# The message product of layer 3: the picks of s are summed before the gathered d rows arrive

## The chip, the cores and the metric

The kernel runs on one NeuronCore of a Trainium2 chip. The time is the device time of one execution in microseconds (us); for the kernel before it is the median of three runs, 1174.64 us (1171.81 to 1176.21). The engines are called PE (TensorE, with PEld for its weight loads), DVE (VectorE), ACT (ScalarE), POOL (GpSimd) and SP (SyncE, which issues most plain transfers).

## The reference, cut to what matters

Four layers run over a graph of 4096 nodes with 128 features, each as `x = x + layer(relu(layernorm(x)))`. The matrix `adj` is 4096 x 4096 and sparse, with uneven rows: a few nodes have many entries. Layers 0 to 2 (neighbour sum, Chebyshev filter, attention) multiply with it or a function of it. Layer 3 computes

```python
s = node_feats @ msg_w[:, :D].T
d = node_feats @ msg_w[:, D:].T
messages = gelu(s[:, None, :] + d[None, :, :] + msg_b)
aggregated = einsum('ijd,ij->id', messages, adj)
```

and then an update (a product, gelu, a layer norm). A message is needed only where `adj[i, j]` is not zero. The kernel makes, for each such entry (row i, column j), the vector `gelu(s_i + d_j)`, and adds it, times the entry's value, into row i.

## The kernel before, in words

**Tiling.** The nodes are put in an order on the host so that rows with many entries come first, and cut into 32 blocks of 128; four blocks are a group of 512 rows, with one PSUM bank as its accumulator. The entries of a block are listed in chunks of 128 entries. Blocks 0 and up have 26 (in four units of 7, 7, 7 and 5), 11, 8, 7, 6, 6, 5 and so on down to 3 chunks, 158 in all. A message of the program is up to four chunks of one unit, and there are 49 of them: two for every unit of 5 to 8 chunks, three for block 1, and one for each of the blocks 10 to 31.

**One message** is the generator `Messages.message`, with `Messages.rows` beside it:

1. `selection` makes a 0/1 matrix that picks, for each entry of a chunk, its row of s: ACT writes distances (L623), DVE compares them (L625), into a lane of `m_lanes`.
2. When s of the group is there (`prepare`), DVE makes `r`, one 128 x 128 tile per chunk (L1403), which will send each entry back to its row, times its value. `r` lives in `r_tiles`.
3. `rows` has POOL gather the rows of d by an indirect DMA (L553), one per chunk, from a table in HBM into the message's buffer `m`. The program waits for all of them (`yield here[q]`).
4. PE adds d and s in a bank: a product of the identity with the gathered rows (L1409, up to 512 columns at once), then one product per chunk with the selection and s (L1411).
5. ACT takes the gelu of the bank into `m` (L1415), and the bank is free.
6. PE multiplies with `r` into the group's accumulator (L1421), and `r` and `m` are free.

In the profile an f32 product on PE shows as two records, so L1409 has 98 and L1411 and L1421 have 316 each.

**A group** starts with `prepare` (s for its rows, L597 and L1370, the diagonal entries, and the accumulator opened by a product of zeros, L602, then L1386). It ends with `finish`: the accumulator is copied (L1433), multiplied with the update weights (L597, `upd_h_sb` and `upd_a_sb`), and goes through a bias (L1441), gelu (L1444) and norm (L1453, L1456, L1458, L1462) to the output. Group 0, with the blocks that have most entries, sums in one of the two `picks` banks, the others in `accs`.

**Buffers.** While layer 2's attention runs there are three `banks`, four message buffers, one selection lane and two r tiles; only messages of block 0 run, at a low rank. When the attention is through, eight halves of its buffers become message buffers (twelve in all), and there are four lanes, four r tiles and one bank more. The d table is written group by group by `finish_3`, when two stripes of the attention are done: a transposition (L588), a product (L597, `msg_d_sb`), a copy and a store. Messages of blocks 1 and up need the whole table.

**The order of the work.** The kernel has no loops at run time. Its parts are Python generators; a planner (`Plan`) lets them go on one at a time, by when they could begin and by rank. A line such as `yield "PE", n * 0.84` asks for an engine with an expected duration (PE's are scaled by 0.72), `yield banks` asks for a buffer, and `yield here[q]` waits for an event, here the expected landing. The code behind the `yield` is then written into the program, and `in_order` keeps each engine's instructions in the planned order. What an engine does on the chip waits for its data in that order. Where the plan has a gap of over 0.8 us on PE and a bank has been free, `fill` puts in products of zeros (L610), up to 80% of the gap.

Of the kernel before, what the change touches and what calls it, by code (L numbers as in the profile page):

```python
# [26 lines left out]
D = 128  # L27
# [4 lines left out]
GB = BANK // D  # L32
# [334 lines left out]
def on_act(n, table=None):  # L367
    return ("ACT", 0.22 + 0.83e-3 * n) + ((table,) if table else ())
# [10 lines left out]
def sparse_stack(tc, x, adj, adjT, diag, w_self, w_neigh, b0, w1, b1, w2, att_src, att_dst,  # L379
# [7 lines left out]
    nc = tc.nc  # L387
    plan = Plan()
    EARLY = 7
    with ExitStack() as ctx:  # L390
# [4 lines left out]
        def tiles(pool, name, n, shape, dtype=F32):  # L395
            return Slots([pool.tile(list(shape), dtype, name=f"{name}{i}", tag=f"{name}{i}") for i in range(n)])

        def kept(name, shape, dtype=F32):
            return keep.tile(list(shape), dtype, name=name, tag=name)
# [17 lines left out]
        banks = tiles(ps, "bank", 3, (P, BANK))  # L417
# [25 lines left out]
        ident = kept("ident", (P, P))  # L443
# [156 lines left out]
        def open_bank(p):  # L600

            nc.tensor.matmul(p, nothing[0:1, :P], nothing[0:1, :], start=True, stop=False)  # L602
# [9 lines left out]
        def rows_of(p, n=GB):  # L612
            return p[:, :n * D].rearrange("p (k d) -> p k d", d=D)
# [6 lines left out]
        def selection(lane, mids, h, g, n):  # L620

            yield on_act(n * P)
            nc.scalar.activation(lane["t"][:, :n * P], iota_row[:, :n * P], AF.Abs, bias=mids[:, g:g + 1])  # L623
            yield on_dve1(n * P)
            nc.vector.tensor_scalar(lane["sel"].rearrange("p q e -> p (q e)")[:, :n * P], lane["t"][:, :n * P], h, None,  # L625
                                    op0=ALU.is_le)
# [690 lines left out]
        class Messages:  # L1317
# [76 lines left out]
            def message(self, g, b, u, c, chunks, m, here):  # L1394
                n = len(chunks)
                yield u_done[u.number]
                lane = yield m_lanes
                yield from selection(lane, mids[:, u.number, :], half[:, u.number:u.number + 1], c, n)
                yield self.s_here[g]
                r = yield r_tiles  # L1400
                yield "DVE", 0.35 * n
                for q, k in enumerate(chunks):
                    nc.vector.tensor_scalar(r[:, q, :], iota_row[:, :P], e_row[:, k:k + 1], e_val[:, k:k + 1],  # L1403
                                            op0=ALU.is_equal, op1=ALU.mult)
                for q in range(n):
                    yield here[q]
                p = yield banks
                yield "PE", n * 0.84
                nc.tensor.matmul(p[:, :n * D], ident, m[:, :n, :], start=True, stop=False)  # L1409
                for q in range(n):  # L1410
                    nc.tensor.matmul(p[:, q * D:(q + 1) * D], lane["sel"][:, q, :], self.s_rows[g][:, b % GB, :],  # L1411
                                     start=False, stop=q == n - 1)
                plan.release(m_lanes, lane)
                yield on_act(n * D, "gelu")
                nc.scalar.activation(m[:, :n, :], rows_of(p, n), AF.Gelu)  # L1415
                plan.release(banks, p)
                yield "PE", 0.42 * n
                acc = self.acc[g]
                for q in range(n):
                    self.left[b] -= 1  # L1420
                    nc.tensor.matmul(acc[:, b % GB * P:(b % GB + 1) * P], m[:, q, :], r[:, q, :], start=False,  # L1421
                                     stop=all(self.left[g * GB + k] == 0 for k in range(GB)))
                plan.release(r_tiles, r)
                plan.release(messages, m)
                if all(self.left[g * GB + k] == 0 for k in range(GB)):
                    plan.start(self.finish(g), -2)
# [160 lines left out]
        for i in range(2):  # L1587
            def lane_tile(name, width, dtype=F32):
                return second.tile([P, width], dtype, name=f"{name}_{i}", tag=f"{name}_{i}")
            lane = {k: lane_tile(k, -(-most // 2) + 2 * GB) for k in ("et", "ev", "epop", "ecum", "evf")}  # L1590
# [3 lines left out]
            n = max(sum(u.cap for u in g.units) for g in GROUPS)  # L1594
# [23 lines left out]
        def message_lanes(pool, numbers):  # L1618
            return [{"t": pool.tile([P, BANK], F32, name=f"mt{i}", tag=f"mt{i}"),
                     "sel": pool.tile([P, GB, P], F32, name=f"msel{i}", tag=f"msel{i}")} for i in numbers]  # L1620
# [11 lines left out]
        m_lanes = Slots(message_lanes(early, range(1)))  # L1632
# [365 lines left out]
```

## Time and profile before

| what | value |
|---|---|
| median of three runs | 1174.64 us |
| the profiled execution | 1485.49 us |
| its span | 1483.4 us, mean clock 0.842 |
| PE busy (share of the span) | 1055.1 us (71%) |
| DVE, ACT, POOL busy | 792.7, 671.2, 766.4 us (53%, 45%, 52%) |
| zero products that open a bank (L602, from 985 us) | 20, median 384 ns |
| zero products that fill (L610, 1205 to 1445 us) | 120, median about 379 ns |
| gathers of d rows (L553) | 158 |

The profiled execution is 311 us longer than the median; its durations of single instructions and its order are used here, and a difference of times is set against its own time first. Times are counted from the start of the span. In the tables an idle time before an instruction is followed by what ended it: "issue" is a wait for nothing that the profile shows, "remote" one for something outside the core. Tile names are those of the program: a message's buffer appears as `m`, or as `e` or `tau` where it is a half of an attention buffer, and a bank as `bank` or `pick`.

### The profile page before, as it was taken

What the parts mean: (1) busy time and instruction counts of PE and PEld (TensorE: products, weight loads), DVE (VectorE), ACT (ScalarE), POOL (GpSimd) and SP (SyncE); (2) the same over time, 40 slices, a digit from 0 to 9 for tenths busy, and PEclk for the clock granted to TensorE, in tenths of its full rate; (3) what the DMA queues carried; (4) which work ended last, traced back from release to release, by engine and by line L of the source; (5) the groups of instructions that cost most, each with busy time, mean ns of one, the idle gap of its engine ahead of it and who ended that gap; (6) DMA issues with size and microseconds to landing.
All of it is one profiled execution on the core that took longest, in us unless ns stands there. A gap on an engine that the chain in (4) does not pass through costs nothing.

```text
span 1483.4 us, 19188 instructions
## 1 busy us (share of the span) xinstructions
PE 1055.1 (71%) x5943; PEld 722.2 (49%) x5943; DVE 792.7 (53%) x2982; ACT 671.2 (45%) x1344; POOL 766.4 (52%) x832
## 2 busy tenths in 40 slices
PE   6786778877486687667677069968767872957774
PEld 2454556554265465455555045534434452645663
DVE  5796567787466476345645048444444451424453
ACT  5983466664021213113335048656555630334366
POOL 4136664344635565546656733765557346664530
PEclk9897799897697899778888579979888995988988
DMA  8999899895565777766544034333333212112210
GB/s 252 357 329 334 286 299 330 305 353 185 135 185 147 211 228 227 201 187 181 150 115 132 8 93 132 107 88 89 88 107 97 61 50 49 42 42 53 61 45 24
DMA packets 175415, 236.03 MB, mean 159 GB/s; under 512 B 22452, under 2 KB 155336, under 8 KB 167112
## 3 DMA queue, kind: packets, MB, share of 16 engines
q1 hardware_dynamic: 148904, 186.45, 37.8%
q0 software_dynamic: 26400, 48.27, 13.6%
q8 instruction: 49, 0.80, 0.2%
q14 instruction: 62, 0.51, 0.1%
HBM read 203.41 MB, written 31.23 MB: 158 GB/s over the span
## 4 chain that ended last, share of the span: by engine, by line
PE 23%; another core or an unknown queue 13%; ACT 10%; DVE 7%; issue 6%; DMA 1%; POOL 0%; ACTq 0%; SPq 0%; DVEq 0%; POOLq 0%
PE acc L1253 4%; PE acc L1255 3%; PE bank L597 2%; PE acc L1421 2%; PE acc L1139 2%; PE acc L1156 2%; ACT junk L1453 1%; ACT e L1229 1%; ACT junk L568 1%; PE bank L1411 1%; PE pick L610 1%; ACT e L1232 1%; PE bank L1409 1%; DVE ehit L891 1%
## 5 line engine op out<-in xcount | busy, mean ns | idle before, releaser
L553 POOL DMA_INDIRECT e_val<-in_adj,e_at x158 | 154.5, 978 | 48.0 <-issue 45.6
L553 POOL DMA_INDIRECT g<-h_tab,fetch_row x136 | 136.1, 1001 | 73.0 <-issue 34.3
L610 PE MATMUL pick<-nothing 128*128 128x512 f16 x536 | 142.9, 416 | 1.6 <-issue 1.6
L1139 PE MATMUL acc<-big,hA 128*128 128x256 f32 x448 | 131.7, 442 | 10.7 <-issue 7.7
L610 PEld LDWEIGHTS <-nothing 128*128 128x128 f16 x795 | 82.9, 107 | 99.3 <-issue 33.4
L553 POOL DMA_INDIRECT g<-a_tab,fetch_col x74 | 76.9, 1039 | 93.6 <-issue 45.3
L553 POOL DMA_INDIRECT rseg<-in_adjT,seg_row x68 | 71.1, 1046 | 103.4 <-issue 28.8
L1139 PEld LDWEIGHTS acc<-big,hA 128*128 128x128 f32 x448 | 96.4, 225 | 28.6 <-issue 9.5
L553 POOL DMA_INDIRECT cseg<-in_adj,seg_col x74 | 70.8, 957 | 63.9 <-issue 23.2
L891 DVE SCALAR_TENSOR_TENSOR ehit<-ehit,pos,pick 128x32 f32<-128x32 f32 (+7 forms) x158 | 38.8, 285 | 116.0 <-issue 80.1
L1236 DVE TENSOR_TENSOR tau<-e,big 128x512 f32<-128x512 f32 (+3 forms) x61 | 54.3, 891 | 85.5 <-ACT e L1232 47.8
L553 POOL DMA_INDIRECT g<-u_tab,fetch_row x68 | 64.6, 950 | 64.9 <-PE acc L1156 37.1
L888 ACT COPY ehit<-pick 128x192 f32<-128x192 f32 (+7 forms) x74 | 20.4, 286 | 154.5 <-remote 80.4
L553 POOL DMA_INDIRECT tau<-d_tab,e_col x63 | 60.6, 962 | 57.2 <-issue 15.0
L769 ACT ACTIVATE mask<-dst 128x2048 fp8e4<-128x2048 f32 x43 | 81.8, 1903 | 14.2 <-DMA dst<-in_adj 8.0
L553 POOL DMA_INDIRECT m<-d_tab,e_col x70 | 68.4, 977 | 38.5 <-issue 17.4
L1156 PE MATMUL acc<-big,g 128*128 128x256 f32 x272 | 80.2, 434 | 0.6 <-DMA big<-r_tab 0.5
L568 ACT ACTIVATE junk<-xN,stat 128x128 f32<-128x128 f32 x128 | 51.4, 401 | 60.0 <-DVE stat L564 27.0
L623 ACT ACTIVATE sel_t<-iota_row,mids 128x512 f32<-128x512 f32 (+3 forms) x43 | 27.1, 642 | 109.7 <-DVE mids L618 63.7
L610 PE MATMUL bank<-nothing 128*128 128x512 f16 x259 | 70.6, 414 | 2.7 <-issue 2.3
L884 PE MATMUL pick<-eA,esel 128*128 128x65 f16 (+7 forms) x158 | 27.0, 245 | 61.4 <-DVE esel L625 28.0
L1139 PE MATMUL acc<-big,hB 128*128 128x256 f32 x224 | 62.7, 420 | 1.7 <-DMA big<-in_adjT 1.7
(331 smaller groups left out, 2717.2 us busy)
## 6 DMA issues: line engine op xcount, KB each, us to landing
dst<-in_adj SPq DMA_DIRECT2D x43, 1024.0 KB
big<-in_adjT SPq DMA_DIRECT2D x45, 512.0 KB
raw<-in_adj SPq DMA_DIRECT2D x21, 1024.0 KB
big<-in_adjT SPq DMA_DIRECT2D x66, 256.0 KB
big<-r_tab SPq DMA_DIRECT2D x30, 512.0 KB
c_tab<-cseg SPq DMA_DIRECT2D x74, 128.0 KB
r_tab<-rseg SPq DMA_DIRECT2D x68, 128.0 KB
big<-c_tab SPq DMA_DIRECT2D x15, 512.0 KB
```

The lines of the kernel that those rows point to most:

```text
L553: nc.gpsimd.indirect_dma_start(out=dst, out_offset=None, in_=table[:, :], in_offset=bass.IndirectOffsetOnAxis(ap=index, axis=0))
L568: nc.scalar.activation(junk, src[:, k, :], AF.Square, bias=st[:, 0, k:k + 1], accum_out=st[:, 1, k:k + 1])
L597: nc.tensor.matmul(p[:, k * D:(k + 1) * D], lhs[:, k * P:(k + 1) * P], w, start=i == 0, stop=i == len(terms) - 1)
L610: nc.tensor.matmul(idle[2][idle[1]], nothing[:, :P], nothing, start=True, stop=True)
L769: nc.scalar.activation(mask[:, h * HALF:(h + 1) * HALF], raw_of[b, h], AF.Sigmoid, scale=1e38, accum_out=marks[:, 2 * b + h:2 * b + h + 1] ...
L891: nc.vector.scalar_tensor_tensor(hit[:, q, :], hit[:, q, :], pos0[:, k + q:k + q + 1], pv[:, q, W:2 * W], op0=ALU.is_le, op1=ALU.mult, acc ...
L1139: nc.tensor.matmul(acc, self.near[:, b, :D], as_rows(t)[:, k, :], start=count == 0, stop=count == every - 1)
L1156: nc.tensor.matmul(acc, row[:, :D], r, start=count == 0, stop=count == every - 1)
L1236: nc.vector.tensor_mul(tau[:, :n, :], e[:, :n, :], a[:, :n, :])
L1253: nc.tensor.matmul(acc[0:1, CS:2 * CS], parts[k][:, D + 1:], tau[:, k, :], start=False, stop=False)
L1255: nc.tensor.matmul(acc[:, :CS], parts[k][:, :D], e[:, k, :], start=False, stop=self.count[s.index] == every - 1)
L1421: nc.tensor.matmul(acc[:, b % GB * P:(b % GB + 1) * P], m[:, q, :], r[:, q, :], start=False, stop=all(self.left[g * GB + k] == 0 for k in ...
```

## The change

In `message`, the bank is asked for right behind `r`, ahead of the wait for the gathered rows. A product of zeros opens it (`open_bank`, the function that opens the accumulators), the products with s are added, and the selection lane is given back. Then the message waits for the gathers, and the product of the identity with the gathered rows comes last. The durations that the planner is told are split: `n * 0.42 + 0.22` for the first part and `n * 0.42` for the second.

```diff
+                p = yield banks
+                yield "PE", n * 0.42 + 0.22
+                open_bank(p)
+                for q in range(n):
+                    nc.tensor.matmul(p[:, q * D:(q + 1) * D], lane["sel"][:, q, :], self.s_rows[g][:, b % GB, :],
+                                     start=False, stop=False)
+                plan.release(m_lanes, lane)
                 for q in range(n):
                     yield here[q]
-                p = yield banks
-                yield "PE", n * 0.84
-                nc.tensor.matmul(p[:, :n * D], ident, m[:, :n, :], start=True, stop=False)
-                for q in range(n):
-                    nc.tensor.matmul(p[:, q * D:(q + 1) * D], lane["sel"][:, q, :], self.s_rows[g][:, b % GB, :],
-                                     start=False, stop=q == n - 1)
-                plan.release(m_lanes, lane)
+                yield "PE", n * 0.42
+                nc.tensor.matmul(p[:, :n * D], ident, m[:, :n, :], start=False, stop=True)
                 yield on_act(n * D, "gelu")
```

`open_bank`, which is not changed:

```python
def open_bank(p):
    nc.tensor.matmul(p, nothing[0:1, :P], nothing[0:1, :], start=True, stop=False)
```

## The prediction

> **What bounds the kernel now.** I read the page's busy times first, then a table by stage, then the order of time on GpSimd (POOL), TensorE (PE) and ScalarE (ACT) in the stages that the edit touches. The first part of the page:
>
> ```profile
> PE 1055.1 (71%) x5943; PEld 722.2 (49%) x5943; DVE 792.7 (53%) x2982; ACT 671.2 (45%) x1344; POOL 766.4 (52%) x832
> ```
>
> No engine is full over the span, so the limits are local. Messages run from about 985 us; three stretches of layer 3 after the attention, from the table by stage (stretch, length, then busy us of PE, PEld, DVE, ACT, POOL, clock, DMA):
>
> ```profile
> 1207.00:1300.00 93.00, 58.31 (x308) 40.60 (x306) 21.19 (x66) 13.67 (x28) 60.19 (x63) 0.80 0.20 48
> 1300.00:1360.00 60.00, 34.86 (x188) 27.84 (x187) 20.22 (x56) 18.57 (x38) 35.67 (x38) 0.80 0.20 50
> 1360.00:1445.00 85.00, 67.13 (x388) 53.30 (x387) 42.98 (x123) 47.20 (x103) 36.44 (x38) 0.88 0.20 52
> ```
>
> A gather keeps POOL for 0.94 us with 0.30 us to the next, a pitch of 1.25. At that pitch the 63 gathers of the first row need 79 of 93 us, the 38 of the last 47.5 of 85. So the gathers set the pace at first and are behind something else at the end. What that is, POOL's order of time says:
>
> ```profile
> 1209.17 0.95 POOL L553 DMA_INDIRECT tau<-d_tab,e_col  x1 [0.30 <-issue]
> ...
> 1369.88 0.98 POOL L553 DMA_INDIRECT m<-d_tab,e_col  x1 [6.86 <-PE acc L1421]
> ...
> 1394.08 1.27 POOL L553 DMA_INDIRECT e<-d_tab,e_col  x1 [7.54 <-PE acc L1421]
> ...
> 1418.15 1.37 POOL L553 DMA_INDIRECT tau<-d_tab,e_col  x1 [7.43 <-PE acc L1421]
> ```
>
> A message buffer comes back only with the closing product L1421, and that is late once per group of four blocks. ACT shows the period, by the table load inside each group's norm:
>
> ```profile
> 1363.51 1.28 ACT L1456 ACT_TABLE_LOAD   x1
> ...
> 1387.40 1.28 ACT L1456 ACT_TABLE_LOAD   x1
> ...
> 1411.58 1.28 ACT L1456 ACT_TABLE_LOAD   x1
> ...
> 1434.12 1.28 ACT L1456 ACT_TABLE_LOAD   x1
> ```
>
> 23.9, 24.2 and 22.5 us apart, where a group's 12 gathers need 12 x 1.25 = 15. So the last groups go round a loop through ACT, PE and DVE, and PE's order inside one turn is:
>
> ```profile
> 1390.99 2.07 PE L1386 MATMUL acc<-r,own 128*128 128x128 f32 x8 [4.52 <-ACT own L1377]
> 1393.01 2.08 PE L1421 MATMUL acc<-r,e 128*128 128x128 f32 x8
> 1394.88 2.68 PE L1421 MATMUL acc<-r,tau 128*128 128x128 f32 x12
> 1397.39 0.81 PE L1409 MATMUL bank<-tau,ident 128*128 128x384 f32 x2
> ```
>
> After that come L1411 (s, six records, 0.66 us to the next) and at 1398.71 the update product L597, which ACT's norm waits for. Earlier, where gathers pace, one message is a d product, s products, fillers, closing product:
>
> ```profile
> 1265.23 1.02 PE L1409 MATMUL bank<-tau,ident 128*128 128x512 f32 x2
> 1266.09 1.05 PE L1411 MATMUL bank<-s,msel 128*128 128x128 f32 x8
> 1266.98 0.81 PE L610 MATMUL bank<-nothing 128*128 128x512 f16 x3
> 1267.83 1.16 PE L1421 MATMUL pick<-r,tau 128*128 128x128 f32 x8
> 1268.82 1.02 PE L1409 MATMUL bank<-m,ident 128*128 128x512 f32 x2
> ```
>
> From start to start: d 0.86, s 0.89, fillers 0.85, closing 0.99, in all 3.59 us for four chunks, against 5.0 us of POOL. An f32 product has two records here: 98 records of L1409 are 49 messages, 316 of L1411 are 158 chunks.
>
> **What the Trainium skill says.** "TensorE: Matmul & The Clock Gate", Part 1, What's actually happening: the array falls to half clock after about 3.4 us of idleness and recovers after as much work. The trace agrees: eight records of L1421 take 1.16 us at 1267.83, and 2.08 at 1393.01 behind a wait of 4.52. So a lost filler can cost as well as save. The same page, Back-to-back issue gap: 512 columns take 512/2.4 + 2.5 = 216 ns warm; 48 fillers take 10.52 us from 1205.90, 219 ns each. "PSUM — Partial Sum Buffer", The four PSUM rules, rule 2: the first product of a group clears the bank's written bits and later ones add; so the zero product lets s and d come in either order. No time in this trace tests that; the accumulators are opened in that way (L602).
>
> **The change part by part.** *Added:* 49 zero products. L602 is the same form, 20 of them with a median of 384 ns: 49 x 0.384 = 18.8 us of PE; bounds 49 x 0.219 = 10.7 (warm, back to back) and 49 x 0.602 (the longest L602) = 29.5. I take 18.8. Most lies in waits for gathers or in place of fillers (L610, 120 records from 1205 to 1445); without that cover it is all cost.
>
> *Moved:* the s products, from behind the gathers' landing to right behind DVE's r (L1403). From landing to gelu a message has 0.89 us (four chunks) or 0.66 (three) less. While POOL paces, this gains nothing: 12 message buffers let POOL run ahead, and PE needs 3.59 + 0.38 = 3.97 of 5.0 us. The s products queue in PE ahead of other messages' d and closing products, and now stand next behind r: three r take 0.85 us on DVE (1394.44 to 1395.3). No DMA is moved, no wait is added on SP or POOL.
>
> *Freed earlier:* the selection lane. Before the attention ends there is one lane, held through the wait for d. With it free the second early message's selection leaves DVE's queue at the end of the attention: 0.29 (L625) + 0.86 (three L1403, from 1187.83), and 0.40 for the third's, ahead of the last stripe's L1284 at 1191.68. That stripe ends in the last d rows, which hold POOL to 1207.92: -1.5 us.
>
> *Held longer:* the bank. Two r tiles before the attention ends mean that two of three banks sit open from about 1000 to 1180 us and the stripes' endings share one. Where two banks overlap in the trace, the later product waits for the earlier one's reader: L1277 at 1114.41 for ACT L590 to 1116.39 (2.0), L588 at 1145.72 for DVE L1288 to 1147.44 (1.7), L588 at 1179.19 for L1288 to 1180.11 (0.9). 4.6 us; PE has idle time there (164.9 busy of 205), so I take +2, bounds 0 and 4.6. Afterwards four r tiles stand against four banks.
>
> *The turn of the late loop.* When the closing products of three messages release their r tiles (1393 to 1397.5), DVE makes three new r at once, and the written order can put three openings and three s sets before L597: 3 x (0.38 + 0.66) = 3.1, less 0.66 for the L1411 that leaves: +2.5 us before the product that ACT waits for. What falls away behind L597 lies beside ACT's norm and gains nothing. Bounds per turn: -0.7 (s all in the wait before L1386) and +3.1. I take +2.5 in four turns: +10.
>
> *The tail.* From 1442.05 PE runs nearly without a break to 1454.3 through seven messages. With four r tiles up to four s sets leave (4 x 0.66 = 2.6) and three openings stay (1.1): about -1.
>
> Sum: 10 + 2 - 1.5 - 1 = +9.5 us. The profiled execution took 1485.49 us (span 1483.4), 311 us above the median of 1174.64; much of that seems to be waits without a visible cause (13% "another core or an unknown queue", 6% "issue" in the chain), so it would go to 1495. I carry the difference over unscaled: 1184 us.
>
> **Rivals.** *Hidden.* POOL's gathers (158 x 1.25 = 197.5 us) hold the pace once the stalls of the profile are gone, PE has room, the early bank conflicts vanish in PE's idle time: -1.5 - 1 + 2 = -0.5 and 1174 us. For it: 3.97 us against 5.0. Against it: the 7 us waits of POOL for L1421. That the planner has no bank free and puts s behind the landing as before ends here too.
>
> *Faster.* In the late loop s goes into the 4.5 us in which PE waits for ACT's own (1386.5 to 1391), and each message's path is shorter by 0.66: four turns x four messages x 0.66 = 10.6, 1164 us. It decides where the order puts s ahead of L1386 instead of L597; two of four turns bring it to the forecast's zero. Against it: the r tiles come free only behind L1386, in L1421.
>
> *Short of banks.* Four waiting messages hold all four banks when a group ends; its ending and the next group's prepare wait for a landing and a gelu, up to three gathers = 3.75 us in each of seven groups: +26, 1200 us. It decides where the fourth message has its r before the ending asks for a bank; the copy of the accumulator (0.58) is shorter than three r (0.85), which speaks against it.
>
> **How the numbers follow.** Forecast 0.38 (own range 1180 to 1194), short of banks 0.07, hidden 0.31, faster 0.24. A change below 0.5%, 5.9 us, can hardly be told from none here. Slower 0.45, same 0.31, faster 0.24. The written order is made anew by the planner from all its due times, so orders elsewhere in layer 3 shift too; this is in the widths. The range reaches to the faster case with three more us, and to the bank shortage: 1161 to 1200.
>
> **What would show it.** Right: 49 more zero products near 0.38 us, L1411 ahead of L1409 in each message; two or three L1411 sets between the last L1421 of a group and L597; table loads L1456 about 2.5 us further apart; fewer L610. Wrong: the same spacing of L1456 (hidden); L1411 inside the wait before L1386 and shorter waits of POOL for L1421 (faster); PE waits of 3 us and more in L597 for ACT's L1415 (banks). The forecast fails if the unprofiled loop is shorter than 15 us a group, since then POOL hides all of it.

## The result, and the profile after

The changed kernel takes 1183.49 us (median of 15 runs, 1178.67 to 1188.91). The kernel before, run beside it, takes 1175.98 us (15 runs, 1171.81 to 1183.72). The ratio is 1.0055, 95% interval 1.0037 to 1.0073: 0.55% slower, some 6.5 us (4.4 to 8.6). Every ratio here leaves out runs more than 1.5% above the fastest run of their kernel; that leaves out hardly any on the chips of usual speed, but many on the slow chips further down, where times spread more widely.

The profile of before that the prediction used is of an execution 311 us above the median. The unchanged kernel was therefore profiled again: 1179.77 us, span 1177.9 us, clock 0.938. The changed kernel's profile has a span of 1181.4 us and a clock of 0.932. All comparisons with "before" below use this second trace of it. Its page begins

```profile
PE 979.2 (83%) x5943; PEld 672.0 (57%) x5943; DVE 794.9 (67%) x2982; ACT 672.2 (57%) x1344; POOL 771.3 (65%) x832
```

and the changed kernel's page begins

```profile
PE 990.0 (84%) x5901; PEld 671.5 (57%) x5901; DVE 792.8 (67%) x2982; ACT 672.6 (57%) x1344; POOL 764.7 (65%) x832
```

PE does 10.8 us more. There are 49 more zero products of one row (L602: 88 records against 39, together 34.4 us against 15.6) and fewer fillers (L610: 704 records against 795). No other engine's busy time differs by more than 7 us. Behind the diff the lines of the changed kernel have moved: the s product is L1409, the d product L1415, the gelu L1417, the closing product L1423, the norm's table load L1458, the memsets that clear the attention's buffers L1648 (L1411, L1409, L1415, L1421, L1456 and L1646 before).

The stages after the attention, from the table by stage of the changed kernel (stretch, length, busy us of PE, PEld, DVE, ACT, POOL, clock, DMA share, GB/s):

```profile
980.00:1060.00 80.00, 66.49 (x367) 44.07 (x367) 33.92 (x102) 27.90 (x58) 60.51 (x64) 0.96 0.26 61
1060.00:1120.00 60.00, 52.96 (x325) 38.47 (x325) 34.11 (x96) 37.53 (x80) 45.67 (x48) 1.00 0.28 69
1120.00:1150.00 30.00, 29.60 (x189) 21.69 (x187) 20.51 (x62) 21.99 (x50) 22.99 (x24) 1.00 0.31 80
```

POOL issues 64 gathers in 80 us, 48 in 60 and 24 in 30: one every 1.25 us, up to the last. In the profile on record the last of these stages had 38 gathers in 85 us. POOL's order of time in the changed kernel:

```profile
957.95 0.93 POOL L553 DMA_INDIRECT e<-d_tab,e_col  x1 [0.30 <-issue]
976.53 0.94 POOL L553 DMA_INDIRECT tau<-d_tab,e_col  x1 [17.65 <-DVE own L1375]
977.78 0.95 POOL L553 DMA_INDIRECT tau<-d_tab,e_col  x1 [0.30 <-issue]
```

One wait stands in it, of 17.65 us, for the last rows of the d table. It ends with the first of the last 137 gathers, and none of the 136 others has a wait of over 0.31 us before it. So the late loop of the recorded profile, with its 7 us waits for the closing product, is absent at this kernel's usual time. It is absent before the change too (one wait of 10.71 us, the same 137 gathers behind it). The table loads of the late groups' norms in the changed kernel agree:

```profile
1095.94 1.28 ACT L1458 ACT_TABLE_LOAD   x1
1113.68 1.28 ACT L1458 ACT_TABLE_LOAD   x1
1129.44 1.28 ACT L1458 ACT_TABLE_LOAD   x1
1145.41 1.28 ACT L1458 ACT_TABLE_LOAD   x1
```

They are 17.7, 15.8 and 16.0 us apart; the same four before are 17.0, 17.0 and 17.0 apart. No such lengthening as the +2.5 us a turn of the prediction is seen. In both kernels 12 to 14 gathers fall between two of these loads, at 1.25 us each: the groups go at the pace of the gathers. A piece of PE's order between them shows the new message:

```profile
1100.98 0.38 PE L602 MATMUL bank<-nothing 1*128 1x512 f16 x1
1101.29 0.94 PE L1409 MATMUL bank<-s,msel 128*128 128x128 f32 x6
1102.06 0.83 PE L1423 MATMUL acc<-r,tau 128*128 128x128 f32 x6
1104.08 0.88 PE L1415 MATMUL bank<-m,ident 128*128 128x384 f32 x2 [1.18 <-DMA m<-d_tab,e_col]
1104.80 0.83 PE L1423 MATMUL acc<-r,tau 128*128 128x128 f32 x6
```

The opening and the s products do stand ahead of the gathered rows, in 1.1 us that PE partly spent waiting before. But PE waits for a gather there in either kernel, so nothing is gained.

**Where the loss is.** The last rows of d come from the attention's last stripe. Its chain in the kernel before, in order of time over the engines:

```profile
939.36 0.49 PE L1277 MATMUL bank<-ident,agg 128*128 128x128 f32 x2 [0.27 <-ACT agg L1272]
940.92 0.17 DVE L1284 RECIPROCAL stat<-bank 128x2 f32<-128x2 f32 x1 [1.67 <-PE bank L1278]
943.44 1.06 ACT L1232 ACTIVATE e<-e 128x1024 f32<-128x1024 f32 x1
944.53 1.23 DVE L1236 TENSOR_TENSOR tau<-e,big 128x1024 f32<-128x1024 f32 x1 [2.79 <-ACT e L1232]
946.54 1.89 PE L1253 MATMUL acc<-tau,g 128*1 128x256 f32 x8
947.08 2.11 DVE L1646 MEMSET e<- 128x512 f32 x4
...
955.27 0.17 DVE L1284 RECIPROCAL stat<-bank 128x2 f32<-128x2 f32 x1
957.06 0.40 ACT L568 ACTIVATE junk<-xN,stat 128x128 f32<-128x128 f32 x1 [2.42 <-DVE stat L564]
962.68 0.60 ACT L1415 ACTIVATE m<-bank 128x512 f32<-128x512 f32 x1
963.17 1.64 ACT L578 ACTIVATE hA<-xN,stat 128x128 f32<-128x128 f32 x4
964.32 0.87 PE L588 MATMUL bank<-ident,hA 128*128 128x128 f32 x4
966.82 1.16 PE L597 MATMUL pick<-msg_d_sb,hT 128*128 128x128 f32 x8 [0.73 <-ACT hT L590]
968.02 0.58 ACT L1305 COPY agg<-pick 128x512 f32<-128x512 f32 x1 [0.76 <-PE pick L597]
971.53 0.95 POOL L553 DMA_INDIRECT tau<-d_tab,e_col  x1 [10.71 <-DVE n_bad L1524]
```

A stripe's sums (L1253, then L1255) are turned by a transposition (L1277) and divided (L1284). L1277 and the first L1284 are those of the stripe before the last, the second L1284 is that of the last. L1232 is the attention's last exponential (the last exp below), L1236 makes from it what the last stripe's products L1253 read. Behind the last L1284 come the norm (L568, L578), the transposition (L588), the product that makes d (L597), the copy, the store, and 2.9 us after the store the first gather. The same chain in the changed kernel:

```profile
943.16 1.06 ACT L1232 ACTIVATE e<-e 128x1024 f32<-128x1024 f32 x1
944.25 1.23 DVE L1236 TENSOR_TENSOR tau<-e,big 128x1024 f32<-128x1024 f32 x1 [5.76 <-ACT e L1232]
946.65 0.49 PE L1277 MATMUL bank<-ident,agg 128*128 128x128 f32 x2 [0.75 <-ACT m L1417]
946.79 1.03 DVE L1648 MEMSET e<- 128x512 f32 x2
948.11 1.89 PE L1253 MATMUL acc<-tau,g 128*1 128x256 f32 x8
951.23 0.48 DVE L1648 MEMSET e<- 128x512 f32 x1 [3.41 <-PE acc L1255]
...
954.66 0.11 DVE L1284 RECIPROCAL stat<-bank 128x2 f32<-128x2 f32 x1
957.77 0.17 DVE L1284 RECIPROCAL stat<-bank 128x2 f32<-128x2 f32 x1
959.54 0.40 ACT L568 ACTIVATE junk<-xN,stat 128x128 f32<-128x128 f32 x1 [4.65 <-DVE stat L564]
963.67 1.64 ACT L578 ACTIVATE hA<-xN,stat 128x128 f32<-128x128 f32 x4
965.22 1.32 ACT L623 ACTIVATE mt<-iota_row,mids 128x512 f32<-128x512 f32 x2
966.55 1.28 ACT L1417 ACT_TABLE_LOAD   x1
967.85 0.98 ACT L1417 ACTIVATE m<-bank 128x512 f32<-128x512 f32 x2
968.50 1.12 PE L588 MATMUL bank<-ident,hA 128*128 128x128 f32 x4 [5.12 <-ACT m L1417]
971.12 1.86 PE L597 MATMUL bank<-msg_d_sb,hT 128*128 128x128 f32 x8
973.01 0.58 ACT L1305 COPY agg<-bank 128x512 f32<-128x512 f32 x1 [2.77 <-PE bank L597]
976.53 0.94 POOL L553 DMA_INDIRECT tau<-d_tab,e_col  x1 [17.65 <-DVE own L1375]
```

Three things have changed. First, the transposition L1277 of the stripe before the last waits for a bank that a block-0 message's gelu still reads; before, it ran at 939.36. It now stands in PE's order right ahead of the last stripe's L1253, which starts 2.6 us after the end of its input L1236; before it was 0.8 us. Second, the earlier stripe's L1284 now stands in DVE's order behind the memsets, some of which wait for the attention's last products (L1255), and beside two sets of r. Together the two make the last stripe's L1284 2.50 us later on the clock of the trace, and L568 with it. Third, ACT now does two selections, a table load and a gelu between L578 and the point where L588 gets its bank. L588 starts 4.83 us after L578 (968.50 - 963.67), where it took 1.15 us (964.32 - 963.17). Before, the gelu stood ahead of L578, which gives back 2.0 us of that. L597 then needs 1.86 us in place of 1.16 behind the wait. The store of the last rows starts at 973.62 instead of 968.63, 5.0 us later.

In these two executions the span's difference is 3.5 us: +5.0 at the store, +0.7 from the last gather to the end (31.4 against 30.7 us), and -2.2 in the gathers between, whose durations differ a little.

### The profile page after: what moved, and what is told of

It is laid out like the page before. It is cut to its first block, busy times and chain, and to the rows that moved or that the text cites. A ratio compares the mean times of both kernels' runs of the same rounds, so it can differ in the third digit from the quotient of the medians.

```text
span 1181.4 us, 19107 instructions
## 1 busy us (share of the span) xinstructions
PE 990.0 (84%) x5901; PEld 671.5 (57%) x5901; DVE 792.8 (67%) x2982; ACT 672.6 (57%) x1344; POOL 764.7 (65%) x832
## 4 chain that ended last, share of the span: by engine, by line
DMA 30%; PE 25%; ACT 13%; DVE 12%; POOL 9%; issue 8%; SPq 0%; POOLq 0%; ACTq 0%; DVEq 0%
DMA dst<-in_adj 5%; POOL e_val L553 4%; DMA cseg<-in_adj,seg_col 4%; PE acc L1139 3%; DMA g<-h_tab,fetch_row 3%; PE acc L1156 3%; PE bank L597 3%; ACT mask L769 3%; POOL g L553 3%; DMA e_val<-in_adj,e_at 3%; PE pick L610 2%; DMA big<-in_adjT 2%; DMA g<-a_tab,fetch_col 2%; ACT junk L568 2%; DMA m<-d_tab,e_col 2%
## 5 line engine op out<-in xcount | busy, mean ns | idle before, releaser
L553 POOL DMA_INDIRECT e_val<-in_adj,e_at x158 | 158.5, 1003 | 48.0 <-issue 40.1
L610 PE MATMUL pick<-nothing 128*128 128x512 f16 x514 | 132.5, 406 | 0.0
L1139 PE MATMUL acc<-big,hA 128*128 128x256 f32 x448 | 118.6, 410 | 8.7 <-DMA big<-in_adjT 5.8
L610 PEld LDWEIGHTS <-nothing 128*128 128x128 f16 x704 | 72.0, 105 | 80.7 <-issue 18.7
L553 POOL DMA_INDIRECT rseg<-in_adjT,seg_row x68 | 67.0, 985 | 74.9 <-issue 27.4
L1139 PEld LDWEIGHTS acc<-big,hA 128*128 128x128 f32 x448 | 88.5, 206 | 22.4 <-DMA big<-in_adjT 6.6
L553 POOL DMA_INDIRECT m<-d_tab,e_col x76 | 73.3, 965 | 23.2 <-issue 15.2
L553 POOL DMA_INDIRECT tau<-d_tab,e_col x63 | 60.8, 965 | 36.6 <-DVE own L1375 17.7
L1236 DVE TENSOR_TENSOR tau<-e,big 128x512 f32<-128x512 f32 (+3 forms) x61 | 54.3, 891 | 41.1 <-ACT e L1232 38.8
L568 ACT ACTIVATE junk<-xN,stat 128x128 f32<-128x128 f32 x128 | 51.3, 401 | 44.0 <-DVE stat L564 32.3
L1156 PEld LDWEIGHTS acc<-big,g 128*128 128x128 f32 x272 | 53.2, 209 | 27.5 <-DMA g<-h_tab,fetch_row 10.0
L1229 ACT ACTIVATE e<-dst,g 128x256 f32<-128x256 f32 x74 | 34.9, 501 | 38.7 <-DMA g<-a_tab,fetch_col 38.2
```

What stands on the lines that cost most here:

```text
L553: nc.gpsimd.indirect_dma_start(out=dst, out_offset=None, in_=table[:, :], in_offset=bass.IndirectOffsetOnAxis(ap=index, axis=0))
L568: nc.scalar.activation(junk, src[:, k, :], AF.Square, bias=st[:, 0, k:k + 1], accum_out=st[:, 1, k:k + 1])
L610: nc.tensor.matmul(idle[2][idle[1]], nothing[:, :P], nothing, start=True, stop=True)
L1139: nc.tensor.matmul(acc, self.near[:, b, :D], as_rows(t)[:, k, :], start=count == 0, stop=count == every - 1)
L1156: nc.tensor.matmul(acc, row[:, :D], r, start=count == 0, stop=count == every - 1)
L1229: nc.scalar.activation(e[:, k, :], dst[:, s.lo:s.lo + CS], AF.Relu, bias=h[:, D:D + 1])
```

## Experiments

Theory A (the prediction): the loss arises in the late groups, where s sets stand ahead of the update product. Theory B, formed from the changed kernel's trace: it arises at the end of the attention, where block-0 messages hold banks in which they have only summed s. Three more: the zero products themselves cost; holding a bank early costs whatever the order; or the time goes into the tail, from the last gather to the end. Ratios are to the kernel before on the same chip.

**before_look**: the kernel before, unchanged, to have a trace at its usual time.

> The kernel before, unchanged, profiled again for a trace that stands near its median. Late-loop theory (the prediction's): POOL still waits some 7 us for L1421 in each of the last groups, so the last gather of d rows ends late because of PE, ACT and DVE. Attention theory: POOL gathers without such waits, as in the changed kernel, and the gathers behind the full d table start 5 to 7 us before the changed kernel's 976.5. Tail theory: they start within 2 us of it, and from the end of the last gather to the end of the span there are 5 to 7 us less than the changed kernel's 31.4.

Measured: 1179.77 us; the readings are those above. The late loop isn't there. The first gather behind the whole table starts 5.0 us before the changed kernel's, as theory B had it, and the tail is 0.7 us shorter, not 5 to 7.

**zero_only**: the kernel before, its bank opened by the product of zeros, in place.

```diff
-                nc.tensor.matmul(p[:, :n * D], ident, m[:, :n, :], start=True, stop=False)
+                open_bank(p)
+                nc.tensor.matmul(p[:, :n * D], ident, m[:, :n, :], start=False, stop=False)
```

> The kernel before with the zero product put in front of d and s, at the same place and with the same expected durations, so that the order of all else is that of before. If PE's 49 x 0.384 = 18.8 us stand on the path: 5 us and more above before, so 1181 and up. If they lie beside the gathers (attention theory, tail theory): within 2 us of before, 1174 to 1178.

Measured: 1177.99 against 1177.74 us, ratio 1.0009 (0.9988 to 1.0031). The 49 zero products (88 records of L602, 34.5 us together) cost nothing that can be measured.

**bank_early**: the kernel before, the bank asked for ahead of the wait, all products behind it.

```diff
+                p = yield banks
                 for q in range(n):
                     yield here[q]
-                p = yield banks
```

> The kernel before with the bank asked for ahead of the wait for the gathered rows, and all products still behind it; no zero product. If the held banks cost the time (attention theory): 5 to 8 us above before, 1181 to 1184. If the early s products or the zero products do: within 2 us of before.

Measured: 1177.76 us, ratio 1.0009 (0.9982 to 1.0036). Holding the bank through the wait costs nothing by itself, in the old order of the work.

**no_zero**: the changed kernel without the zero product; the first s product opens the bank.

```diff
-                open_bank(p)
                 for q in range(n):
                     nc.tensor.matmul(p[:, q * D:(q + 1) * D], lane["sel"][:, q, :], self.s_rows[g][:, b % GB, :],
-                                     start=False, stop=False)
+                                     start=q == 0, stop=False)
```

> The changed kernel without the zero product: the first s product of a message opens the bank (start), the others write their own columns; expected durations and order as in the changed kernel. If the zero products cost the time: back to 1175 to 1178. If the order and the buffers do: still 1181 to 1185.

Measured: 1184.02 us, ratio 1.0050 (1.0029 to 1.0070). The loss stays whole. Its order of time repeats both signs, the late L1277 and the wait of L588:

```profile
943.85 0.49 PE L1277 MATMUL bank<-ident,agg 128*128 128x128 f32 x2 [0.75 <-ACT m L1416]
...
965.70 1.12 PE L588 MATMUL bank<-ident,hA 128*128 128x128 f32 x4 [5.64 <-ACT m L1416]
```

So the loss needs the earlier s with the early bank, and not the zeros.

**hub_old**: the changed kernel, but the messages of block 0 in the old form. **hub_new**: the reverse, only those in the new form. **bank4**: the changed kernel with the second bank of the picks given to the shared banks from the start of layer 3's messages, and not only after the attention. **hub_wait**: the kernel before, its block-0 messages held back until the whole d table is there. The diffs are those of hub_old (hub_new has `if not b`), bank4 and hub_wait.

```diff
+                if b:
+                    p = yield banks
+                    yield "PE", n * 0.42 + 0.22
+                    open_bank(p)
...
+                else:
+                    for q in range(n):
+                        yield here[q]
+                    p = yield banks
+                    yield "PE", n * 0.84
...
```

```diff
         last = Messages()
+        more_of(banks, [picks.items[picks.free.pop()[1]]])
```

```diff
+                if not b:
+                    yield d_here[NC - 1]
                 lane = yield m_lanes
```

> The changed kernel, but messages of block 0 (the only ones that run before the attention is through) in the form of before; all others, from block 1 on, in the new form. If the loss is made at the attention's end (attention theory: banks held by block 0's messages make the last stripe's endings wait): 1174 to 1179, and POOL's wait for the full d table is 10 to 13 us as before, not 17.7. If it is made in the late groups (the prediction's step): still 1181 to 1185.

> The opposite: only messages of block 0 in the new form. Attention theory: 1181 to 1186, and POOL waits about 17 us for the full d table. Late-group theory: within 3 us of before.

> The changed kernel, with the second picks bank given to the banks when layer 3's messages begin, instead of after the attention: four banks for three in that stretch, no other edit. If the lack of banks causes the loss: L588 and L1277 of the last stripes no longer wait for ACT's L1417, POOL waits 10 to 13 us for the d table, 1174 to 1179. If the place of the selections and gelus in ACT's and DVE's order causes it: 1181 to 1185.

> The kernel before, with the messages of block 0 told to wait for the last d rows before their selection, so that nothing of theirs stands among the last stripe's endings (they come later, beside the gathers of the other blocks). If the messages' work delays the last d rows in before too: POOL's wait for the full table falls from 10.7 to 5 to 8 us and the time to 1170 to 1174. If their buffers come back too late for the next gathers, POOL waits later instead: 1176 and more.

Measured, on a chip where the kernel before takes 1523.22 us: ratios 1.0025 (0.9900 to 1.0149), 1.0104 (0.9971 to 1.0236), 1.0005 (0.9893 to 1.0117) and 1.0097 (0.9997 to 1.0197). None settles anything: each interval is wider than the effect. POOL's wait for the last d rows was 16.7, 18.9, 13.9 and 11.2 us, against 13.9 us in the profile of before on record, which is of like speed. The long one of hub_old stands against theory B; those of hub_new and bank4 are for it. hub_wait's is shorter (5 to 8 us was expected), but no gain in time shows. That the eight messages held back still have to be made afterwards may be why; it was not tested.

**hub_old_b** and **bank4_b**: the same two kernels on a chip where the kernel before takes 1177.4 us.

> The changed kernel with the messages of block 0 in the old form (wait, selections, bank, d, then s), all others in the new form; repeated on another chip. Attention's end: block-0 messages are the only ones that hold banks there, so the wait for the last rows of d is back at 10-13 us and the time at 1174-1179 us. Late loop (each of the later messages holds its bank longer): the loss stays, 1181-1186 us.

> The changed kernel with the second bank of the picks given to the shared banks once attention has ended its use of them, repeated on another chip because the first try left the question open. Shortage of banks at the attention's end (the last stripe's transpositions wait for a bank that a block-0 message still holds until its gelu has read it): with one more bank that wait shrinks, GpSimd's wait for the last rows of d comes down from 17 to 10-13 us, and the time is 1174-1179 us against about 1176 for the kernel before. If the loss is the order of the other engines' work and not the banks: wait still 16-18 us and time 1181-1185 us.

Measured: hub_old_b 1178.78 us, ratio 1.0013 (0.9986 to 1.0039); bank4_b 1176.54 us, ratio 0.9997 (0.9971 to 1.0024). With block 0 alone in the old form, most of the loss is gone, though 41 of the 49 messages are still in the new form. That speaks against theory A; its interval and that of the changed kernel just touch (1.0037 to 1.0039). With the one more bank all of it is gone, and the intervals don't meet. In hub_old_b's order of time the transposition L588 follows without a wait of its own, and POOL's wait is near that of before:

```profile
959.56 1.16 PE L1434 MATMUL pick<-r,m 128*128 128x128 f32 x8 [2.12 <-ACT m L1428]
960.56 0.87 PE L588 MATMUL bank<-ident,hA 128*128 128x128 f32 x4
...
968.30 0.97 POOL L553 DMA_INDIRECT tau<-d_tab,e_col  x1 [11.82 <-DVE r L1381]
```

In bank4_b the earlier stripe's L1284 is back ahead of the memsets, and L588 waits half as long:

```profile
947.51 0.17 DVE L1284 RECIPROCAL stat<-bank 128x2 f32<-128x2 f32 x1 [1.68 <-PE bank L1278]
953.65 2.11 DVE L1649 MEMSET e<- 128x512 f32 x4
...
972.09 1.11 PE L588 MATMUL bank<-ident,hA 128*128 128x128 f32 x4 [2.71 <-ACT m L1417]
```

(This profiled execution took 1187.45 us, 11 us above the median of its kernel, so only distances within the chain are read from it; POOL's wait in it was 14.1 us, above the 10 to 13 expected.)

The start of the last exp, ACT's L1232, is a common zero for the chains. From it, in us, to the starts of the chain's steps, each from one profiled execution (a minus is a start ahead of the exp):

| kernel | ratio of times | L1277, stripe before the last | last stripe's L1253 | last L1284 | L588 | L597 (d) | first gather behind |
|---|---|---|---|---|---|---|---|
| before | 1 | -4.08 | 3.10 | 11.82 | 20.88 | 23.38 | 28.09 |
| zero_only | 1.0009 | -4.08 | 3.10 | 11.88 | 20.91 | 23.41 | 28.13 |
| bank_early | 1.0009 | -2.16 | 3.10 | 11.66 | 20.69 | 23.72 | 28.33 |
| hub_old_b | 1.0013 | -4.07 | 3.10 | 11.82 | 21.39 | 24.53 | 29.14 |
| bank4_b | 0.9997 | -4.08 | 4.43 | 10.78 | 22.06 | 24.68 | 29.69 |
| no_zero | 1.0050 | 3.49 | 4.95 | 14.61 | 25.34 | 27.96 | 33.04 |
| changed | 1.0055 | 3.49 | 4.94 | 14.60 | 25.34 | 27.95 | 33.36 |

Only in the two kernels that lose time does the earlier stripe's L1277 come behind the last exp, and their stretch is 5.0 and 5.3 us longer than before; the four that lose nothing clear of noise have it within 1.6 us. hub_old_b's 1.05 us stands beside a time 1.4 us longer; bank4_b's 1.6 us has no loss beside it, and its trace is of an execution above its median. So theory B is borne out. The 5.3 us lie within the interval of the loss (4.4 to 8.6 us), below its middle of 6.5. What comes ahead of the last exp can't be laid to the change: where that falls varies from 935.3 to 950.0 us between these executions.

**hub_new_b** and **before_bank4**: only the block-0 messages in the new form again, and the kernel before with the one more bank (the diff of bank4).

> Only the messages of block 0 in the new form, all others in the old: these are the messages that run beside the end of attention. If the loss arises there, it is all kept: 1181-1186 us, GpSimd's wait for the last rows of d near 17 us. If it arises in the later messages, this kernel is at the time of the kernel before, 1174-1179 us, with a wait of 10-13 us.

> The kernel before with the one more bank given to the shared banks after attention has ended its own use of it. If banks at the attention's end only run short in the new order, nothing changes: 1174-1179 us and a wait of 10-13 us for the last rows of d. If the old order too waits there for a bank, the wait shrinks to 5-9 us and the time falls to 1168-1173 us.

Measured, on another chip where the kernel before takes long (1485.23 us, from 1460.02 to 1515.06): hub_new_b 1489.42 us, ratio 1.0090 (1.0057 to 1.0123); before_bank4 1481.60 us, ratio 0.9902 (0.9852 to 0.9952). Absolute times can't be held against the expectations there, and the ratios only with care: the medians of all runs are only 0.28% above and 0.24% below that of before. So a loss with the eight messages of block 0 alone is likely, but its size isn't known, and a gain from the fourth bank in the kernel before isn't shown.

hub_new_b's trace has one of the two signs, the late L1277; L588 follows L578 there within 1.2 us, without the long wait:

```profile
1173.06 1.06 ACT L1232 ACTIVATE e<-e 128x1024 f32<-128x1024 f32 x1
...
1176.55 0.80 PE L1277 MATMUL bank<-ident,agg 128*128 128x128 f32 x2
```

The earlier stripe's L1277 again starts behind the last exp, by 3.5 us. From that exp to the first gather behind the table it is 32.9 us, against 27.9 in the profile on record and 29.0 in before_bank4's: 3.9 to 5.0 us more. hub_new's trace, on the other slow chip, has 32.2. POOL's wait in hub_new_b is 19.6 us, near 17 as expected. In before_bank4 the wait is 14.5 us against 13.9 in the profile on record, so no shortening by the fourth bank is seen. Whether before_bank4 is better than both kernels stays open; it was not run on a chip of the usual speed.

## Why the prediction was right, and where it was wrong

The number holds: 1184 forecast, 1183.49 measured. That it does is luck, for most of its working doesn't hold: the sum came out by a step that isn't there and one that was far too small.

- **The late loop (+10) failed.** It was the main term. No gather waits for a closing product in either kernel at its usual time, and the table loads are not further apart. The slow turns were a property of the execution profiled, and the prediction's last sentence named the danger: without a loop slower than the gathers, POOL hides all of it. In place of the profiled 22.5 to 24.2 us a turn took 17.0 before and 15.8 to 17.7 after, near the pace of its 12 to 14 gathers. Carrying a loss from an execution 311 us too long "unscaled" to the median was the wrong step; the stage should have been asked whether it could still be that slow at the median.
- **The bank held through the wait (+2, bounds 0 and 4.6): right in kind, too small.** The prediction looked for the conflicts between stripes all through the attention. What counts is the last one. L1277 made the last stripe's L1253 1.8 us later, counted from its input. L588's distance from L578 grew by 3.7 us (4.83 against 1.15), because the bank's reader, a gelu behind a table load and two selections, is late in ACT's order. PE's own idle time, given there as cover, is none: all gathers of blocks 1 and up wait for the result.
- **The lane freed earlier (-1.5): not seen.** Selections were to leave DVE's queue ahead of the last stripe's L1284. Instead the stripe before the last lost its bank, its own ending moved behind the memsets, and the last L1284 came 2.8 us later, counted from the last exp. These two terms, +0.5 together, measured +5.3 in the chain.
- **The zero products (18.8 us of PE, hidden): right.** 18.8 us more of L602 were measured, and zero_only shows no cost.
- **The s products moved ahead: right** that they gain nothing while POOL paces; the gathers follow at 1.25 us in both kernels.
- **The tail (-1; its own figures, 2.6 and 1.1, give -1.5): not told apart.** From last gather to end it is 30.7 us before and 31.4 after, while the other profiles of usual speed have 28.9 to 33.9.
- **The rivals.** "Hidden" had the late stages right: the gathers hold the pace. It failed where it let the early bank conflicts vanish in PE's idle time. "Short of banks" named the right resource in the wrong place: 26 us over seven late groups, where it costs about 5.3 us once, at the attention's end. "Faster" did not occur: there was no loop for it to shorten.

On what the Trainium skill said: "TensorE: Matmul & The Clock Gate", Part 1, has the array fall to half clock after idleness. The changed kernel agrees: behind the idle 5.12 us before L588 the eight records of L597 took 1.86 us, against 1.16 before, and this lies on the path. "PSUM — Partial Sum Buffer", The four PSUM rules, rule 2, says that the first product of a group clears the written bits of the whole bank, not its data, and that later products overwrite where the bit is clear and add where it is set. no_zero leans on this, with an s product of 128 columns as the first: leaving out the 49 zero products won nothing, 1184.02 against 1183.49 us.

## What to carry to other kernels

Ask of a buffer that is asked for earlier not how long it is held, but which last use of the same pool everything else waits for, and what stands ahead of its reader on the reader's engine. A reordering in a planned program moves the work of other engines too: here the waits showed on PE, but they ended with a gelu that stood late in ACT's order. Before a loss is priced from a profile that is far slower than the median, check from the stage's own pace whether the stall can exist at the median.

## What was not expected of the hardware

The kernel before takes about 1177 us on two chips and 1485 and 1523 us on two others. In hub_new_b's trace the granted clock is 0.846 where the traces of usual speed have 0.92 to 0.94: 8 to 10% less, beside a time 26% longer. In hub_new_b's and hub_new's traces POOL's gathers wait up to 8.3 us for closing products late in layer 3, as in the profile on record, and none do on the usual chip. What makes those chips slow wasn't looked into.
